# A gated cross-attention kernel: the last product of its setup split by a second Strassen step, and part of the setup's storing moved into the main loop

## The chip, the cores and the metric

The kernel runs on one core of a Trainium2 chip. The metric is the device time of one execution in microseconds (us); less is better. The time before is the median of three runs, 972.33 us (972.21 to 972.43). One further execution was recorded by the hardware profiler; every duration of a single instruction comes from there.

## The reference

All arrays are float32. Eight batches of 1024 rows x of width 1024 attend to 64 rows of memory of width 512.

```python
memory_proj = jnp.einsum('bme,de->bmd', memory, W_mem)            # "mp", 512 rows in all
scores = jnp.einsum('bnd,bmd->bnm', hidden_states, memory_proj) / jnp.sqrt(jnp.float32(D))
attn = jax.nn.softmax(scores, axis=-1)
memory_context = jnp.einsum('bnm,bmd->bnd', attn, memory_proj)
gate_input = jnp.concatenate([hidden_states, memory_context], axis=-1)
gate = jax.nn.sigmoid(jnp.einsum('bnf,df->bnd', gate_input, W_gate) + b_gate)
fused = hidden_states + gate * memory_context
return _rmsnorm(fused, norm_w)
```

W_gate acts on x by its first half, W1 (1024 x 1024), and on the context by its second half, W2. As the context is attn times mp, the kernel computes mp times W2 once ("mg", 512 x 1024) and uses attn times mg.

## The kernel before, in words

**Setup.** The weights and the memory are loaded; mp is computed, transposed, as four quarters m11, m12, m21, m22 (tiles mpT, each 128 x 4 x 256) by seven half-size products after Strassen (tiles pm). Then mg is computed from the quarters and from W2's eight tiles w2 (b11, b12, b21, b22 are column halves of four tiles each), again by seven products in Strassen's (Winograd's) form, in the order 1, 6, 5, 2, 7, 4, 3 (`mg_product`, `mg_sum`, tiles pg; lines 511 to 589). One such product is 8 matmuls of 128x512, into two PSUM banks. `setup_bank` (line 235) hands the eight banks out in turn. VectorE adds the products from PSUM into c11, c12, c21, c22, and `store_mg` writes these to a DRAM scratch tensor mgd[1]. The last product, 3, is s2 times b22 and goes into c12 alone. Between the products stand, by hand, the steps that prepare the main loop:

- `store_mp` (492, called at 550): for each of the four groups of 128 rows of mp, two VectorE transposes of 128x512 into a tile mpq, then four stores of 128 KB to mgd[0]. The mpq tiles take the tags it4, it6, it2, it3.
- `inner_sum` / `inner_sums` (217 to 224): for each of W1's seven outer operands (1 to 7), four sums of 128x512 that a second Strassen step needs, written to a tile it{o} and in place. Before the change GpSimd makes those of sets 1 (328), 7 (541), 5 (564), 6 and 4 (572); VectorE makes those of sets 2 and 3 in the first quad (645 to 648).
- `w2_sum` (321): b21 minus t2 on VectorE (569), four sums of 128x512, an operand of product 4.
- loading and transposing the first 512 rows of x (`load_xq`, `transpose_x`), and their first sums (`outer_s`, `inner_s`).

**Main loop.** A quad is 512 rows of x; there are 16, two to a batch (QPB = 2). A quad's product with W1 is seven outer products in the order 1, 6, 7, 5, 4, 2, 3 (`ORDER`), and each is seven inner products A, B, C, D, (A again), E, F of two matmuls of 128x256 (`outer_product`, line 758). An outer product has five banks for its kA to kF, and they rotate from one outer product to the next (898): kC takes the bank that kA of the outer product before had. Product A is copied out by ScalarE (815), and, for outer product 1, once more when its second half is in (810). The other sums are VectorE's (from PSUM) and GpSimd's (SBUF only). The last four outer products also add attn times mg (`ext`).

**Order of the work.** Every engine executes its instructions in the order of the program (`pin`). The steps beside the products are placed by hand: each inner product is a slot, a quad has 49, `at(slot, ...)` puts a step ahead of a slot, `mid` inside an outer product (`plan`, 607). Loads and stores other than the accumulating ones go through SyncE's queue (SP) in order. At a batch's start, `load_mg` (467) loads 64 rows of mgd[0] and mgd[1] into the tile mg, `load_mp` (463) those of mp, transposed, into the tile mpb, ten slots into the quad before.

**Buffers.** The pool `small` has one buffer for each tag. Tag junk is used by s3 in the setup (540), and in the quads by `square` (670): ScalarE squares a finished tile of 128 x 1024 into it, only for the sum. The squares of a quad's second row pair come in slots 3 and 4 of the next quad, those of the first pair in slots 17 and 18.

Of the kernel before, what the change touches and what calls it, by code (L numbers as in the profile page):

```python
# [8 lines left out]
F32 = mybir.dt.float32  # L9
AF = mybir.ActivationFunctionType  # L10
ALU = mybir.AluOpType
# [4 lines left out]
P = 128  # L16
# [4 lines left out]
def tile_gated_cross_attention_rmsnorm(  # L21
# [42 lines left out]
    nc = tc.nc  # L64
    B, N, D = x.shape
    M, E = mem.shape[1:]
    QT = 4 * P
    QPB = N // QT
    NQ = B * QPB
    BM = B * M  # L70
    KD = D // P
    KE = E // P
    H = 512
    C = 256
    NPAIR = BM // P
    SCALE = 1.0 / float(D) ** 0.5
    Q4 = D // 4

    const = ctx.enter_context(tc.tile_pool(name="const", bufs=1))
# [4 lines left out]
    small = ctx.enter_context(tc.tile_pool(name="small", bufs=1))  # L84
# [4 lines left out]
    pin = tc.keep_in_program_order  # L89

    def mm(o, lhsT, rhs, start, stop):
        pin(nc.tensor.matmul(o, lhsT, rhs, start=start, stop=stop, skip_group_check=True))  # L92

    def tt(eng, o, a, b, op):
        pin(eng.tensor_tensor(o, a, b, op))  # L95

    def load(o, i):
        pin(nc.sync.dma_start(o, i))

    def t4k(pool, shape, tag, name):  # L100
        return pool.tile(shape, F32, tag=tag, name=name)
# [5 lines left out]
    def chunks(t, n):  # L107

        return t.rearrange("p s e -> p (s e)").rearrange("p (m j) -> p j m", j=n)
# [26 lines left out]
    for k in range(KD):  # L136
        t = t4k(*((gpool, [P, D], "gate") if k < 7 else (apool, [P, D], "s4")), f"w2_{k}")
# [28 lines left out]
    def w1_place(o):  # L166

        if o in (5, 6, 4):
            outer_b[o] = const.tile([P, 4, H], F32, tag=f"t{o}", name=f"t{o}")
        inner_t[o] = const.tile([P, 3, 2, C], F32, tag=f"it{o}", name=f"it{o}")  # L170

    def w_op(o, s):
        if s >= T4:
            return inner_t[o][:, s - T4, :, :]
        k, n = {R11: (0, 0), R21: (1, 0), R12: (0, 1), R22: (1, 1)}[s]
        return outer_b[o][:, 2 * k : 2 * k + 2, n * C : (n + 1) * C]
# [8 lines left out]
    mgd = dram.tile([2, BM, D], F32, name="mgd")  # L185
# [31 lines left out]
    def inner_sum(eng, o, n):  # L217
        s, a, b = ((T1, R12, R11), (T2, R22, T1), (R12, R22, R12), (T4, R21, T2))[n]
        tt(eng, w_op(o, s), w_op(o, a), w_op(o, b), ALU.subtract)

    def inner_sums(eng, o):
        w1_place(o)
        for n in range(4):
            inner_sum(eng, o, n)
# [3 lines left out]
    KH = KD // 2  # L228
    HM = BM // 2
    mpT = [[t4k(apool, [P, KH, HM], f"a{r + 1}{h + 1}", f"mpT{r}{h}") for h in range(2)] for r in range(2)]  # L230
# [4 lines left out]
    def setup_bank(name):  # L235
        nonlocal setup_next
        tag = setup_banks[setup_next % 8]
        setup_next += 1
        return (ps_ctx if tag == "ctx" else ps).tile([P, H], F32, tag=tag, name=name)
# [54 lines left out]
    for k in range(2):  # L294
        pin(nc.scalar.copy(pw22[:, k], w22[:, k]))
    pgs = pm_product(2, w12, e21)
# [12 lines left out]
    pgs = pm_product(7, ps3, e12)  # L309
# [4 lines left out]
    b11, b12, b21, b22 = (  # L314
        [w2[h * KH + k][:, c * H : (c + 1) * H] for k in range(KH)]
        for h in range(2)
        for c in range(2)
    )
    t1, t2 = ([t[:, k, :] for k in range(KH)] for t in t_w2)

    def w2_sum(eng, o, a, b):
        for k in range(KH):
            tt(eng, o[k], a[k], b[k], ALU.subtract)
# [1 line left out]
    w2_sum(nc.gpsimd, t1, b12, b11)  # L325
    w2_sum(nc.gpsimd, t2, b22, t1)
    w2_sum(nc.gpsimd, b12, b22, b12)
    inner_sums(nc.gpsimd, 1)

    pgs = pm_product(3, ps4, e22)  # L330
    pm_sum(m21, m21, pgs)
# [4 lines left out]
    sTs, attns, attnTs, scs, mps, mgs = {}, {}, {}, {}, {}, {}  # L336
# [3 lines left out]
    def transpose_x(q, t, half):  # L340

        key = q, t // 2, half
        if key not in A:
            A[key] = t4k(
                apool, [P, KH, 2 * P], f"a{t // 2 + 1}{half + 1}", f"a{t // 2 + 1}{half + 1}_{q}"
            )
        r = t % 2
        pin(
            nc.vector.transpose(  # L349
                A[key][:, :, r * P : (r + 1) * P],  # L350
                chunks(xq[q][:, 4 * t : 4 * t + 4, :], KD)[:, half * KH : (half + 1) * KH],
            )
        )

    def outer_s(q, n):
        a11, a12, a21, a22 = (A.get((q, r, h)) for r in range(2) for h in range(2))
        if n == 3:
            S[q, 3] = a21
            tt(nc.vector, a21, a11, a21, ALU.subtract)
            return  # L360
        s = S[q, n] = t4k(apool, [P, KH, 2 * P], f"s{n}", f"s{n}_{q}")
        if n == 1:
            tt(nc.vector, s, a21, a22, ALU.add)
        elif n == 2:
            tt(nc.vector, s, S[q, 1], a11, ALU.subtract)
        else:
            tt(nc.vector, s, a12, S[q, 2], ALU.subtract)
# [13 lines left out]
    def quarters(l):  # L381
        return l[:, 0:2, 0:P], l[:, 2:4, 0:P], l[:, 0:2, P:], l[:, 2:4, P:]
# [106 lines left out]
        tt(eng, t, a, b, op)  # L489
        return t  # L490

    def store_mp(g):

        r, n = g // 2, g % 2
        mpq = const.tile([P, 4, Q4], F32, tag=f"it{(4, 6, 2, 3)[g]}", name=f"mpq{g}")
        for h in range(2):
            pin(
                nc.vector.transpose(
                    chunks(mpq, KD)[:, h * KH : (h + 1) * KH],
                    mpT[r][h][:, :, n * P : (n + 1) * P],  # L500
                )
            )
        for i in range(4):
            load(
                mgd[0, g * P : (g + 1) * P, i * Q4 : (i + 1) * Q4].rearrange(
                    "(s c) e -> c s e", c=32
                ),
                mpq[32 * i : 32 * (i + 1), :, :],
            )

    def mg_product(n, l, r):
        pgs = []
        for t in range(2):
            pg = setup_bank(f"pg{n}_{t}")
            for k in range(KH):
                mm(pg, l[:, k, t * P : (t + 1) * P], r[k], k == 0, k == KH - 1)
            pgs.append(pg)
        return pgs

    def mg_tile(pool, tag, name):  # L520
        return t4k(pool, [P, 2, H], tag, name)

    def mg_sum(o, a, pgs):
        for t in range(2):
            tt(nc.vector, o[:, t, :], a[:, t, :], pgs[t], ALU.add)
# [8 lines left out]
    s2 = mp_step(nc.vector, "s2", apool, s1, m11, ALU.subtract)  # L534
# [3 lines left out]
    outer_sum(7, 3, 7)  # L538
    w1_place(7)
    s3 = mp_step(nc.gpsimd, "junk", small, m11, m21, ALU.subtract)  # L540
    for n in range(4):
        inner_sum(nc.gpsimd, 7, n)
    c11 = mg_tile(rot, "u", "mg_c11")
    c12 = mg_tile(rot, "u", "mg_c12")
    c21 = mg_tile(rot, "l2", "mg_c21")
    c22 = mg_tile(small, "mg", "mg_c22")
    pgs = mg_product(1, m11, b11)
    for t in range(2):
        pin(nc.scalar.copy(c11[:, t, :], pgs[t]))
    for g in (2, 3, 0, 1):  # L550
        store_mp(g)
    load_mp(0)
    pgs = mg_product(6, s2, t2)
    mg_sum(c21, c11, pgs)
# [5 lines left out]
    pgs = mg_product(5, s1, t1)  # L560
# [1 line left out]
    w1_place(6)  # L562
    outer_sum(6, 3, 5)
    for n in range(4):
        inner_sum(nc.gpsimd, 5, n)
    pgs = mg_product(2, m12, b21)
    mg_sum(c11, c11, pgs)
    store_mg(c11, 0, 0)
# [8 lines left out]
    pgs = mg_product(7, s3, b12)  # L577
# [3 lines left out]
    pgs = mg_product(4, m22, b21)  # L581
    mg_sum(c21, c21, pgs)
    store_mg(c21, 1, 0)
    for t in (2, 3):
        transpose_x(0, t, 1)
    outer_s(0, 1)
    pgs = mg_product(3, s2, b22)
    mg_sum(c12, c12, pgs)
    store_mg(c12, 0, 1)
    outer_s(0, 2)  # L590
    load_mg(0)
# [5 lines left out]
    def at(slot, fn, *args):  # L597
        due.setdefault(slot, []).append(lambda: fn(*args))
# [8 lines left out]
    def plan(q):  # L607
        t0 = SLOTS * q
        nxt = q + 1 < NQ
        order = [o for o, _ in ORDER]  # L610
        for i, o in enumerate(order):
            for part, t in ((0, 1), (1, 2 if o == 7 else 5)):
                if i + 1 < len(order):
                    at(t0 + 7 * i + t, inner_s, q, order[i + 1], part)
                elif nxt:
                    at(t0 + 7 * i + t, inner_s, q + 1, order[0], part)
        if q == 0:
            at(t0 + 7, scores, q)
        at(t0 + (6 if q else 7), outer_s, q, 3)
        at(t0 + (20 if q else 7), outer_s, q, 4)  # L620
        at(t0 + 9, transpose_scores, q)
        at(t0 + 10, softmax_a, q)
        at(t0 + 13, softmax_b, q)
        at(t0 + 18, transpose_attn, q)
        at(t0 + 21, attn_difference, q)
        if not nxt:
            at(t0 + 5, load_last)
            return
        at(t0 + 2, load_xq, q + 1)
        for t in (2, 3):  # L630
            mid((q, 5), transpose_x, q + 1, t, 0)
            mid((q, 2), transpose_x, q + 1, t, 1)
        for i, t, half in ((36, 0, 0), (38, 1, 0), (42, 0, 1), (43, 1, 1)):
            at(t0 + i, transpose_x, q + 1, t, half)
        mid((q, 3), scores, q + 1)
        mid((q, 3), outer_s, q + 1, 1)
        mid((q, 3), outer_s, q + 1, 2)
        if (q + 1) % QPB == 0:
            at(t0 + 10, load_mp, (q + 1) // QPB)
            at(t0 + 49, load_mg, (q + 1) // QPB)  # L640
        if q == 0:
            at(t0 + 8, add_bias, mgs[0][M:P, :])
            at(t0 + 20, add_bias, mgd[1, M:, :])
# [290 lines left out]
```

## Time and profile before

| | |
|---|---|
| median of three runs | 972.33 us |
| the profiled execution: its own time | 972.56 us |
| its span in the trace | 970.8 us |
| TensorE matmuls busy | 959.5 us, 4986 records |
| VectorE busy | 818.4 us |
| GpSimd busy | 761.1 us |
| ScalarE busy | 328.5 us |
| granted TensorE clock | 0.996 |
| mg's products in the trace | 33.4 to 81.5 us |
| one quad | 54.85 us |

In the profile, PE is TensorE's matmuls, PEld its weight loads, DVE is VectorE, ACT ScalarE, POOL GpSimd, SP SyncE. A line of the timeline gives start, duration, engine, source line, operation, written tile <- read tiles, shape, and how many instructions were merged. One float32 matmul of the program appears as two records. Where a helper such as `tt` (line 95) or `mm` (line 92) issues the instruction, all its calls have the helper's line, and the tile names tell them apart. A bracket at the end is idle time of the engine just before, and what the profile takes to have ended it.

### The profile page before, as it was taken

What the parts mean: (1) busy time and instruction counts of PE and PEld (TensorE: products, weight loads), DVE (VectorE), ACT (ScalarE), POOL (GpSimd) and SP (SyncE); (2) the same over time, 40 slices, a digit from 0 to 9 for tenths busy, and PEclk for the clock granted to TensorE, in tenths of its full rate; (3) what the DMA queues carried; (4) which work ended last, traced back from release to release, by engine and by line L of the source; (5) the groups of instructions that cost most, each with busy time, mean ns of one, the idle gap of its engine ahead of it and who ended that gap; (6) DMA issues with size and microseconds to landing.
All of it is one profiled execution on the core that took longest, in us unless ns stands there. A gap on an engine that the chain in (4) does not pass through costs nothing.

```text
span 970.8 us, 14402 instructions
## 1 busy us (share of the span) xinstructions
PE 959.5 (99%) x4986; PEld 774.9 (80%) x4986; DVE 818.4 (84%) x1482; ACT 328.5 (34%) x604; POOL 761.1 (78%) x889
## 2 busy tenths in 40 slices
PE   9999999999999999999999999999999999999995
PEld 8646878788888888788888888888887878888884
DVE  6988879879797988979797978979797978979787
ACT  2000234161423334161433324152333425152345
POOL 4997878778786978878786978878687878878692
PEclk9999999999999999999999999999999999999998
DMA  9856573482919374482918375381917465391712
GB/s 378 271 141 163 98 131 98 114 169 72 178 66 166 97 144 105 108 176 66 184 65 159 102 137 113 95 188 55 195 67 146 115 129 121 87 196 48 189 69 86
DMA packets 70919, 128.32 MB, mean 132 GB/s; under 512 B 12352, under 2 KB 49216, under 8 KB 70592
## 3 DMA queue, kind: packets, MB, share of 16 engines
q1 hardware_dynamic: 61520, 93.34, 37.0%
q0 software_dynamic: 9184, 33.56, 18.9%
q8 instruction: 39, 0.64, 0.3%
q10 hardware_dynamic: 144, 0.52, 0.1%
q14 instruction: 32, 0.26, 0.1%
HBM read 87.56 MB, written 41.68 MB: 133 GB/s over the span
## 4 chain that ended last, share of the span: by engine, by line
PE 98%; DVE 1%; issue 0%; ACT 0%; DVEq 0%
PE kA L92 20%; PE pc L92 12%; PE kE L92 11%; PE kD L92 10%; PE kF L92 10%; PE kB L92 10%; PE kC L92 10%; PE psT L92 6%; PE pg L92 5%; PE pm L92 3%; PE pz L92 0%; PE pa L443 0%; PE sc L417 0%; PE pt L196 0%; DVE gate L749 0%
## 5 line engine op out<-in xcount | busy, mean ns | idle before, releaser
L95 POOL TENSOR_TENSOR gate<-gate,u 128x256 f32<-128x256 f32 x336 | 287.5, 887 | 107.5 <-DVE u L95 107.5
L662 ACT ACTIVATE gate<-gate 128x512 f32<-128x512 f32 x128 | 80.5, 631 | 306.9 <-DVE gate L95 306.1
L349 DVE STREAM_TRANSPOSE a<-xq 128x512 f32<-128x512 f32 x128 | 137.9, 1099 | 2.7 <-POOL it L95 2.7
L95 POOL TENSOR_TENSOR l<-a 128x256 f32<-128x256 f32 x128 | 122.0, 953 | 21.6 <-PE kA L92 20.4
L92 PE MATMUL pc<-mg,attnT 64*128 64x256 f32 x512 | 127.5, 389 | 0.0
L92 PE MATMUL kB<-it,l 128*128 128x256 f32 x448 | 115.1, 379 | 0.2 <-DVE gate L95 0.2
L92 PE MATMUL kD<-it,l 128*128 128x256 f32 x448 | 115.0, 379 | 0.0
L92 PEld LDWEIGHTS pc<-mg,attnT 64*128 64x128 f32 x512 | 90.6, 186 | 29.9 <-issue 21.2
L691 DVE SCALAR_TENSOR_TENSOR gate<-gate,ss,nw_sb 128x512 f32<-128x512 f32 x120 | 110.6, 931 | 1.1
L95 POOL TENSOR_TENSOR l<-s 128x256 f32<-128x256 f32 x96 | 78.0, 813 | 36.1 <-PE kF L92 35.9
L92 PE MATMUL kA<-w,a 128*128 128x256 f32 x384 | 98.6, 379 | 0.0
L92 PEld LDWEIGHTS kB<-it,l 128*128 128x128 f32 x448 | 85.0, 190 | 12.1 <-DVE gate L95 0.6
L92 PEld LDWEIGHTS kD<-it,l 128*128 128x128 f32 x448 | 85.1, 190 | 11.6
L95 DVE TENSOR_TENSOR gate<-gate,pc 128x512 f32<-128x512 f32 x128 | 86.7, 678 | 0.4 <-ACT gate L662 0.4
L95 DVE TENSOR_TENSOR gate<-gate,kE 128x256 f32<-128x256 f32 x112 | 45.5, 419 | 47.1 <-PE kE L92 41.1
L92 PEld LDWEIGHTS kA<-w,a 128*128 128x128 f32 x384 | 71.7, 190 | 9.5 <-DVE s L95 0.2
L815 ACT COPY u<-kA 128x256 f32<-128x256 f32 x112 | 40.5, 361 | 110.3 <-PE kA L92 106.0
L92 PE MATMUL kE<-it,a 128*128 128x256 f32 x256 | 69.0, 392 | 0.0
L676 ACT ACTIVATE junk<-gate 128x1024 f32<-128x1024 f32 x60 | 63.5, 1058 | 10.5 <-DMA gate<-in_x 9.5
L92 PE MATMUL kA<-t,s 128*128 128x256 f32 x256 | 65.8, 379 | 0.0
L92 PE MATMUL kC<-w,l 128*128 128x256 f32 x256 | 65.7, 379 | 0.0
L92 PE MATMUL kF<-w,l 128*128 128x256 f32 x256 | 65.7, 379 | 0.0
(140 smaller groups left out, 2041.0 us busy)
## 6 DMA issues: line engine op xcount, KB each, us to landing
xq<-in_x SPq DMA_DIRECT2D x64, 512.0 KB, 10.3
gate<-in_x POOLq DMA_DIRECT2D x60, 512.0 KB, 8.1
out<-gate SPq DMA_DIRECT2D x60, 512.0 KB, 2.6
w<-in_w_gate_t SPq DMA_DIRECT2D x8, 512.0 KB, 10.0
w<-in_w_gate_t SPq DMA_DIRECT2D x2, 2048.0 KB, 17.1
mg<-mgd SPq DMA_DIRECT2D x16, 256.0 KB, 3.8
mpd<-mpT SPq DMA_DIRECT2D x4, 512.0 KB, 7.0
mgd<-mpq SPq DMA_DIRECT2D x16, 128.0 KB, 3.6
```

Of the source, the lines that this page charges most:

```text
L92: pin(nc.tensor.matmul(o, lhsT, rhs, start=start, stop=stop, skip_group_check=True))
L95: pin(eng.tensor_tensor(o, a, b, op))
L349: nc.vector.transpose(A[key][:, :, r * P : (r + 1) * P], chunks(xq[q][:, 4 * t : 4 * t + 4, :], KD)[:, half * KH : (half + 1) * KH],)
L662: pin(nc.scalar.activation(g, g, AF.Sigmoid))
L676: nc.scalar.activation(junk, O[q, t], AF.Square, accum_out=ss[:, t % 2 : t % 2 + 1])
L691: nc.vector.scalar_tensor_tensor(g[:, cols], g[:, cols], rstd[:, t % 2 : t % 2 + 1], nw_sb[:, cols], ALU.mult, ALU.mult,)
L815: pin(nc.scalar.copy(p1, kb["A"]))
```

## The change

1. Product 3 of mg (s2 times b22, into c12) is made by a second Strassen step, `mg_nested`: twelve sums of 128x256 on GpSimd for its inputs (eight of b22's tiles, four of s2; they lie in buffers it2 and it3, whose W1 sums are made only in the quads), seven products of two matmuls of 128x256 into six banks, one ScalarE copy and three VectorE additions for the partial sums (tile mg_u, tag junk), three GpSimd additions into c12 and four VectorE additions into c12. The function is a generator run in three parts, with other work between.
2. Of mp's rows only group 0, the rows of batches 0 and 1, is transposed and stored in the setup (`store_mp_pair`). Those of batches 2 to 7 are made at slot 49 of the quad before the batch, that is, slot 0 of its first quad (`store_mp_batch`): one VectorE transpose of 128x512 from mpb into a tile mpq with tag junk, then four stores of 64 KB. `load_mg` moves one slot later and stands behind them.
3. W1's sums of sets 7 and 5 move from GpSimd to VectorE. Those of set 1 stay on GpSimd and move behind s3.

```diff
-    inner_sums(nc.gpsimd, 1)
...
-    def store_mp(g):
-
-        r, n = g // 2, g % 2
-        mpq = const.tile([P, 4, Q4], F32, tag=f"it{(4, 6, 2, 3)[g]}", name=f"mpq{g}")
+    def store_mp(mpq, rows):
+
+        for i in range(4):
+            load(
+                mgd[0, rows, i * Q4 : (i + 1) * Q4].rearrange("(s c) e -> c s e", c=32),
+                mpq[32 * i : 32 * (i + 1), :, :],
+            )
+
+    def store_mp_pair():
+        mpq = const.tile([P, 4, Q4], F32, tag="it4", name="mpq")
         for h in range(2):
             pin(
                 nc.vector.transpose(
-                    chunks(mpq, KD)[:, h * KH : (h + 1) * KH],
-                    mpT[r][h][:, :, n * P : (n + 1) * P],
+                    chunks(mpq, KD)[:, h * KH : (h + 1) * KH], mpT[0][h][:, :, :P]
                 )
             )
...
+        store_mp(mpq, slice(0, P))
+
+    def store_mp_batch(b):
+        mpq = t4k(small, [P, M // 32, Q4], "junk", f"mpq{b}")
+        pin(nc.vector.transpose(chunks(mpq, KD), mps[b]))
+        store_mp(mpq, slice(b * M, (b + 1) * M))
...
+    def mg_nested(eng, l, r, ts, ss, o):
+
+
+        l11, l12, l21, l22 = quarters(l)
+        s1_, s2_, s3_, s4_ = (ss[:, i] for i in range(4))
+        t1_, t2_, t3_, t4_ = (ts[i] for i in range(4))
+        lo, hi = slice(0, C), slice(C, H)
+        for k in range(2):
+            tt(eng, t1_[:, k, :], r[k][:, hi], r[k][:, lo], ALU.subtract)
+            tt(eng, t2_[:, k, :], r[2 + k][:, hi], t1_[:, k, :], ALU.subtract)
+            tt(eng, t3_[:, k, :], r[2 + k][:, hi], r[k][:, hi], ALU.subtract)
+            tt(eng, t4_[:, k, :], r[2 + k][:, lo], t2_[:, k, :], ALU.subtract)
+        tt(eng, s1_, l21, l22, ALU.add)
+        tt(eng, s2_, s1_, l11, ALU.subtract)
+        tt(eng, s3_, l11, l21, ALU.subtract)
+        tt(eng, s4_, l12, s2_, ALU.subtract)
+        yield
...
+        kb = [setup_bank(f"pn{i}")[:, :C] for i in range(6)]
+        ut = t4k(small, [P, 4, C], "junk", "mg_u")
+        p1_, u2, u3, u4 = (ut[:, i, :] for i in range(4))
...
+        product(0, l11, r11)
+        pin(nc.scalar.copy(p1_, kb[0]))
+        product(1, s2_, t2_)
+        add(u2, p1_, kb[1])
+        product(2, s3_, t3_)
+        add(u3, u2, kb[2])
+        for n in (3, 2):
+            tt(nc.gpsimd, dst[n], dst[n], u3, ALU.add)
+        product(3, s1_, t1_)
+        add(u4, u2, kb[3])
+        tt(nc.gpsimd, dst[1], dst[1], u4, ALU.add)
+        product(0, l12, r21, False)
+        product(4, l22, t4_)
+        product(5, s4_, r22)
+        yield
+        for n, b in ((0, 0), (3, 3), (2, 4), (1, 5)):
+            add(dst[n], dst[n], kb[b])
...
     s3 = mp_step(nc.gpsimd, "junk", small, m11, m21, ALU.subtract)
-    for n in range(4):
-        inner_sum(nc.gpsimd, 7, n)
+    inner_sums(nc.gpsimd, 1)
...
-    for g in (2, 3, 0, 1):
-        store_mp(g)
+    store_mp_pair()
+    for n in range(4):
+        inner_sum(nc.vector, 7, n)
     load_mp(0)
...
     outer_sum(6, 3, 5)
     for n in range(4):
-        inner_sum(nc.gpsimd, 5, n)
+        inner_sum(nc.vector, 5, n)
...
+    nested = mg_nested(
+        nc.gpsimd, s2, b22, [in_it2[:, 0], in_it2[:, 1], in_it2[:, 2], in_it3[:, 0]], ss3, c12
+    )
+    next(nested)
     pgs = mg_product(2, m12, b21)
...
+    next(nested)
     outer_s(0, 1)
-    pgs = mg_product(3, s2, b22)
-    mg_sum(c12, c12, pgs)
+    for _ in nested:
+        pass
     store_mg(c12, 0, 1)
...
         if (q + 1) % QPB == 0:
             at(t0 + 10, load_mp, (q + 1) // QPB)
-            at(t0 + 49, load_mg, (q + 1) // QPB)
+            if q + 1 > QPB:
+                at(t0 + 49, store_mp_batch, (q + 1) // QPB)
+            at(t0 + 50, load_mg, (q + 1) // QPB)
```

More of the change, by code (lines that the diff above doesn't have):

```diff
@@ L498, in store_mp @@
                 nc.vector.transpose(
-                    chunks(mpq, KD)[:, h * KH : (h + 1) * KH],
-                    mpT[r][h][:, :, n * P : (n + 1) * P],
-                )
-            )
[L503 to L509, printed above, removed]
+                    chunks(mpq, KD)[:, h * KH : (h + 1) * KH], mpT[0][h][:, :, :P]
+                )
+            )
+        store_mp(mpq, slice(0, P))
[3 more added lines that the diff above has]
+        store_mp(mpq, slice(b * M, (b + 1) * M))
     def mg_product(n, l, r):
@@ L518, in mg_product, with product, add @@
         return pgs
+    def mg_nested(eng, l, r, ts, ss, o):
[13 more added lines that the diff above has]
+        yield
+        r11, r22 = ([r[2 * h + k][:, n] for k in range(2)] for h, n in ((0, lo), (1, hi)))
+        r21 = [r[2 + k][:, lo] for k in range(2)]
+        t1_, t2_, t3_, t4_ = ([t[:, k, :] for k in range(2)] for t in (t1_, t2_, t3_, t4_))
+        kb = [setup_bank(f"pn{i}")[:, :C] for i in range(6)]
+        ut = t4k(small, [P, 4, C], "junk", "mg_u")
+        p1_, u2, u3, u4 = (ut[:, i, :] for i in range(4))
+        def product(n, left_, right_, start=True):
+            for k in range(2):
+                mm(kb[n], left_[:, k, :], right_[k], start and k == 0, k == 1)
+        dst = [o[:, t, n * C : (n + 1) * C] for t in range(2) for n in range(2)]
+        def add(to, a, b):
+            tt(nc.vector, to, a, b, ALU.add)
+        product(0, l11, r11)
[15 more added lines that the diff above has]
+            add(dst[n], dst[n], kb[b])
     def mg_tile(pool, tag, name):
@@ L564, in tile_gated_cross_attention_rmsnorm @@
     for n in range(4):
-        inner_sum(nc.gpsimd, 5, n)
+        inner_sum(nc.vector, 5, n)
+    in_it2, in_it3 = (
+        const.tile([P, 3, 2, C], F32, tag=f"it{o}", name=f"mg_it{o}") for o in (2, 3)
+    )
+    ss3 = in_it3[:, 1:].rearrange("p a k c -> p (a k c)").rearrange("p (i k m) -> p i k m", i=4, k=2)
+    nested = mg_nested(
+        nc.gpsimd, s2, b22, [in_it2[:, 0], in_it2[:, 1], in_it2[:, 2], in_it3[:, 0]], ss3, c12
+    )
+    next(nested)
     pgs = mg_product(2, m12, b21)
```

## The prediction, written before the changed kernel was run

> **What bounds the kernel now.** I read the page first: busy shares, then the chain that ended last.
>
> ```profile
> PE 959.5 (99%) x4986; PEld 774.9 (80%) x4986; DVE 818.4 (84%) x1482; ACT 328.5 (34%) x604; POOL 761.1 (78%) x889
> ...
> PE 98%; DVE 1%; issue 0%; ACT 0%; DVEq 0%
> ```
>
> TensorE is busy in 959.5 of 970.8 us and makes up 98% of the chain. So a matmul taken away is time gained, and anything that makes TensorE wait is time lost. VectorE and GpSimd have room on average only, so I read the stages that the change touches: the setup (30 to 90 us), then the start of a quad that opens a new batch. The timeline of the setup:
>
> ```profile
> 52.74 4.10 DVE L349 STREAM_TRANSPOSE a<-xq 128x512 f32<-128x512 f32 x4 [2.74 <-POOL it L95]
> ...
> 61.55 6.19 DVE L95 TENSOR_TENSOR w<-w,t_w 128x512 f32<-128x512 f32 x4
> ...
> 67.61 7.03 PE L92 MATMUL pg<-w,mpT 128*128 128x512 f32 x16
> ...
> 74.48 7.03 PE L92 MATMUL pg<-w,mp_s 128*128 128x512 f32 x16
> ...
> 78.67 2.19 DVE L95 TENSOR_TENSOR s<-a,a 128x1024 f32<-128x1024 f32 x1
> ...
> 83.07 1.03 PE L92 MATMUL kC<-w,l 128*128 128x256 f32 x4
> ```
>
> VectorE is the neighbour of the bound here: it waits once (2.74 us before 52.74) and is full otherwise. The four w sums make b21 for product 4, which starts at 67.61; they end at 67.74.
>
> The start of quad 4, on ScalarE, then TensorE, then VectorE (the quads that open batches 2 to 7 start alike, within 0.03 us):
>
> ```profile
> 306.50 1.06 ACT L676 ACTIVATE junk<-gate 128x1024 f32<-128x1024 f32 x1
> ...
> 307.68 1.06 ACT L676 ACTIVATE junk<-gate 128x1024 f32<-128x1024 f32 x1
> ...
> 308.85 1.28 ACT L681 ACT_TABLE_LOAD   x1
> ...
> 310.35 0.35 ACT L810 COPY gate<-kA 128x256 f32<-128x256 f32 x1
> ```
>
> ```profile
> 312.98 1.03 PE L92 MATMUL kC<-t,l 128*128 128x256 f32 x4
> ```
>
> ```profile
> 305.26 0.42 DVE L95 TENSOR_TENSOR gate<-gate,kF 128x256 f32<-128x256 f32 x1 [0.44 <-PE kF L92]
> 305.60 0.68 DVE L95 TENSOR_TENSOR gate<-gate,pc 128x512 f32<-128x512 f32 x1
> ```
>
> ScalarE squares two finished tiles into the buffer with tag junk, takes the root, and only then copies kA out of PSUM. The banks rotate so that kC of the next product (6) takes that bank. The copy ends at 310.70, kC comes at 312.98: 2.28 us of room. The stores that the change moves, from the view of the tile mpq and the DMA view of 53 to 58 us:
>
> ```profile
> L98 SPq DMA_DIRECT2D mgd<-mpq x16: 303/430/522, 43.3 to 56.3; - x16
> ...
> DMA to landing us min/median/max: 2.4/3.6/9.6
> ```
>
> ```profile
> mgd<-mpq SPq DMA_DIRECT2D x8, 128.0 KB, 2.6
> ```
>
> 0.43 us to issue one, and 2.6 us to land where the DMA engines are not full.
>
> [...] no mpq store landed in under 2.4 us, so a smaller store is not a much quicker one. [...] w sums beside a busy GpSimd took 6.19/4 = 1.55 us, sums of the same size at 84.48 with GpSimd idle took 0.68. [...] In the trace each engine's instructions follow the program's order, so what is behind a waiting one waits too.
>
> **The change, part by part.**
>
> *TensorE.* Product 3 was 16 records of 0.429 us = 6.87 us. Seven small products replace it, each 0.864 us (kB at 82.21 to kC at 83.07): 6.05 us. Gain 0.82 us, on the path.
>
> *VectorE in the setup.* Six of eight mpq transposes go (0.96 us each, 7.70/8); eight 128x512 sums of sets 7 and 5 come. One such sum costs 0.68 us (GpSimd idle) to 1.55 (the w sums). I take 1.1, half of the 2.19 of the 128x1024 sum at 78.67, which also had GpSimd busy. The four of set 7 are free: two transposes, four sums even at 1.55, and product 6's sums (1.29) take 9.4 us from 41.19, ending at 50.6, before the data of xq let VectorE go on at 52.74. The four of set 5 come after that point and before the w sums: +4.4 us. Last w sum then ends at 67.74 + 4.4 = 72.1; its first use is product 4's fourth pair of records, at 67.61 + 3 x 0.86 = 70.2. TensorE waits 2.0 us there. Further on, VectorE was done with the sum s at 80.78; now 4.4 later, plus three additions of partial products ahead of s (3 x 0.42) and the first last addition to c12 (0.42): 86.9. That addition frees the bank that kC of quad 0 takes. TensorE would be there at 74.48 + 2.0 + 6.05 + 1.73 = 84.3 and waits for 86.9. So kC starts 86.9 - 83.07 = 3.8 us later than before; this net shift already holds the 0.82 gained and the wait at product 4. The ends: 0.68 a sum gives +2.1, 1.55 gives +5.6. A gain is excluded unless xq lands earlier.
>
> *GpSimd in the setup.* Eight sums of 1.27 go (10.2 us); twelve inputs and three additions of 128x256 come, 15 x 0.72 to 0.95 = 11 to 14 us; set 1 moves behind s3. Priced at nothing: the inputs are started at about 58 and end by 70, product 3's place is 77; if that cover goes, each us late is a us of TensorE. The bank kC waits for needs no GpSimd addition. ScalarE's one extra copy (0.37) meets an idle engine.
>
> *SP in the setup.* 12 stores of 128 KB go, 5.2 us of issue; the first loads of mp and x keep their place. Nothing on the path.
>
> *Batch starts.* Six times, VectorE transposes one mpb (1.10, as for xq) right behind the kF sum: 305.60 to 306.70. The following VectorE work is pushed by 1 us, and 0.71 + 0.31 + 0.98 of its idle time in the next 5 us takes that up. SP then issues four stores of 64 KB: the last at 306.70 + 0.05 + 3 x 0.43 = 308.05. Their price is not in the trace at this size: lower end 2.4 (least of the 128 KB ones), upper 3.6 (their median, most of them beside full DMA engines). I take 2.6, for the load of x is now behind them and does not compete. They land at 310.65. The transposed rows lie in the buffer with tag junk, so ScalarE's first square, free to go at 306.50 before, waits for all four stores. Behind it in ScalarE's queue are the second square, the root with its table, the copy of kA, and the next product's copy. First square to end of the kA copy is 310.70 - 306.50 = 4.20, so the bank is free at 314.85; TensorE comes at 312.98 and waits 1.87 us. Ends: 1.7 to 2.9. Six of them: 11.2 us (10.2 to 17.3).
>
> *SP at batch starts.* The load of mg, and the load of x behind it, wait for the stores: mg issued at 310.7 instead of 299.69, x from 311.7. The last x part lands about 313.3 + 10.5 (its median in that window) = 323.8; VectorE wants it at 328.52 + 1.9. mg is wanted at 327.97. Covered by 6 us; were x later than that, each us would reach TensorE through VectorE.
>
> **Sum.** Against the profiled execution's own 972.56 (span 970.8 and 1.76 around it): + 3.8 + 11.2 = 987.6. The median of the runs, 972.33, is 0.2 lower: 987.3.
>
> **The rivals.**
> 1. *Setup covered, batch starts as priced.* [...] xq, with fewer stores beside it, lands 2 us earlier. Against: the stores beside it were mostly issued after it. 972.3 + 11.2 - 0.8 = 982.7.
> 2. *Stores or x land late.* The read and accumulate of x by GpSimd's DMAs (issued 306.7 and 308.3, 11.5 us to land in that window) share the engines with the stores: 3.6 to land, 2.9 us of wait, 17.3 in all, setup at its upper end: 995.2; x landing at its longest (18.3 us in the whole trace) would add over 1 us each.
> 3. *Not slower: DMAs land early.* If the stores release ScalarE by 312.98 - 4.20 = 308.8, that is within 0.7 us of the last issue, the batch starts cost nothing, and xq in by 50.6 leaves 1.7 us of the setup: 974.0. It decides at that 0.7 us; no store in the trace is near it.
> 4. *Batch starts covered, setup as priced:* 972.3 + 3.8 = 976.1.
>
> **How the numbers follow.** Forecast 0.64; rival 1 0.14; rival 2 0.12; rival 3 0.04; rival 4 0.06. The rivals 3 and 4 lie below 979 (0.10), part of rival 2 above 996 (under 0.07), so the range is 979 to 996. About 0.2% is what a measurement of this kernel can tell from no change (970.4 to 974.3). Faster 0.01, same 0.05 (rival 3 and a little of the others), slower 0.94.
>
> **What would show it.** In the profile after: ScalarE's junk square waiting some 4 us for a DMA at quads 4, 6, 8, 10, 12, 14, and kC of product 6 some 2 us late right after, with no such gap at odd quads; TensorE waits near 70 and before kC of quad 0 for VectorE; pn matmuls of 6.05 us together. I am wrong if the squares start within 2.3 us of their old place, if VectorE reaches the c12 additions before 83, or if TensorE waits elsewhere, for xq above all.

## The result and the profile after

| | before | changed | ratio, 95% interval |
|---|---|---|---|
| median | 972.38 us (6 runs) | 1019.87 us (1017.67 to 1021.43, 6 runs) | 1.0488 [1.0477, 1.0499] |
| profiled execution | 972.56 us, span 970.8 | 1017.67 us, span 1015.8 | |

The changed kernel is 47.5 us slower: 1019.87 us, where 987.3 was forecast, with a range to 996. The direction was right; the forecast rise of 15 us was under a third of the real one.

The page of the changed kernel: the shares of busy time, and the chain that ended last.

```profile
PE 975.3 (96%) x4998; PEld 783.8 (77%) x4998; DVE 828.6 (82%) x1495; ACT 328.5 (32%) x605; POOL 766.0 (75%) x896
...
PE 80%; DMA 8%; DVE 4%; POOL 3%; issue 3%; ACT 2%; SPq 1%; DVEq 0%; ACTq 0%; POOLq 0%
```

Two things are to be seen. TensorE has fallen from 98% of the chain to 80%, and DMA, which was not in the chain at all, has 8%. And TensorE is busy 15.8 us longer (959.5 before) though its work became smaller: it must have run slower at times. The granted clock, averaged over the run, is 0.983 (0.996 before).

Where the 45.0 us of span lie can be read from the starts of psT, the scores, once in a quad, in the chain in order of time. To the psT in quad 0, 2.2 us are added, and the psT of the next quad stands at 137.36 instead of 135.08 us (+2.28). Six intervals between two psT, those that hold a batch start with stores, take 61.59 to 62.50 us instead of 54.85 to 55.04: together +42.5. The other intervals are unchanged, and the stretch behind the last psT grows by 0.2. So six batch starts cost 7.1 us each, where 1.9 was forecast, and the setup costs 2.3, where 3.8 was forecast.

The start of quad 4, ScalarE and then TensorE, answering to the lines at 306.50 to 310.35 and at 312.98 of before (this run is 2.3 us later here):

```profile
314.39 1.06 ACT L741 ACTIVATE junk<-gate 128x1024 f32<-128x1024 f32 x1 [5.50 <-DMA mgd<-mpq]
...
318.24 0.35 ACT L875 COPY gate<-kA 128x256 f32<-128x256 f32 x1
```

```profile
318.73 2.05 PE L92 MATMUL kC<-t,l 128*128 128x256 f32 x4 [3.30 <-ACT gate L875]
320.57 1.61 PE L92 MATMUL kD<-it,l 128*128 128x256 f32 x4
322.01 1.03 PE L92 MATMUL kA<-t,s 128*128 128x256 f32 x4
...
333.26 0.91 PE L92 MATMUL kB<-it,l 128*128 128x256 f32 x3 [1.36 <-DVE gate L95]
```

The forecast wait is there: the square waits for the mpq stores, and kC of product 6 for the copy behind it. But it is 3.3 us, not 1.87. Then kC and kD start 1.84 and 1.44 us apart, where each product of this size took 0.86 before: a slow TensorE costs 1.55 us more. And 11 us later TensorE waits again, at kB of product 5, for VectorE. What VectorE waited for stands in the chain in order of time:

```profile
310.35 3.94 DMA mgd<-mpq
...
323.36 9.00 DMA out<-gate
```

The first line is the last of the four mpq stores: 3.94 us to land. The second is a store of a finished tile (the "out store" from here on), 9.00 us to land; only then is its gate buffer free for VectorE's next sums:

```profile
332.45 0.42 DVE L95 TENSOR_TENSOR gate<-gate,kA 128x256 f32<-128x256 f32 x1 [2.53 <-DMA out<-gate]
```

The same store in the kernel before, and VectorE's use of the buffer behind it, without a wait:

```profile
out<-gate SPq DMA_DIRECT2D x1, 512.0 KB, 4.9
```

```profile
322.04 0.42 DVE L95 TENSOR_TENSOR gate<-gate,kA 128x256 f32<-128x256 f32 x1
```

The clock is in the view by stretches (stretch, length, busy time of PE, PEld, DVE, ACT, POOL, granted clock, DMA share, GB/s). Of the stretch behind the first wait, part was at half the clock (granted clock 0.50 from 318.32 to 321.73):

```profile
320.00:325.00 5.00, 5.00 (x20) 4.24 (x20) 4.06 (x11) 0.58 (x2) 3.63 (x5) 0.83 1.15 191
325.00:330.00 5.00, 5.00 (x25) 4.36 (x25) 4.13 (x7) 4.26 (x8) 4.92 (x7) 1.00 1.17 198
```

Quad 4 is one of six such starts. At the others the first wait is 3.34 to 3.54 us, the slow products behind it lose 1.8 to 3.1 us, and the second wait is 0.1 to 1.8 us. Over all six: 20.5 us of first wait, 12.9 of slow clock, 5.5 of second wait. These three can't simply be added up as causes, as the experiments show.

### The profile page after: what moved, and what is told of

It is laid out like the page before. It is cut to its first block, busy times and chain, and to the rows that moved or that the text cites. A ratio compares the mean times of both kernels' runs of the same rounds, so it can differ in the third digit from the quotient of the medians.

```text
span 1015.8 us, 14492 instructions
## 1 busy us (share of the span) xinstructions
PE 975.3 (96%) x4998; PEld 783.8 (77%) x4998; DVE 828.6 (82%) x1495; ACT 328.5 (32%) x605; POOL 766.0 (75%) x896
## 4 chain that ended last, share of the span: by engine, by line
PE 80%; DMA 8%; DVE 4%; POOL 3%; issue 3%; ACT 2%; SPq 1%; DVEq 0%; ACTq 0%; POOLq 0%
PE kA L92 16%; PE pc L92 12%; PE kE L92 9%; PE kC L92 9%; PE kD L92 9%; PE kB L92 8%; PE kF L92 8%; PE psT L92 6%; DMA out<-gate 5%; PE pm L92 2%; DMA mgd<-mpq 2%; POOL mg_it L95 2%; DMA xq<-in_x 1%; POOL it L95 1%; ACT junk L741 1%
## 5 line engine op out<-in xcount | busy, mean ns | idle before, releaser
L95 POOL TENSOR_TENSOR l<-a 128x256 f32<-128x256 f32 x128 | 117.1, 915 | 24.5 <-PE kA L92 20.9
L92 PE MATMUL kD<-it,l 128*128 128x256 f32 x448 | 119.5, 391 | 0.0
L92 PEld LDWEIGHTS kD<-it,l 128*128 128x128 f32 x448 | 88.1, 197 | 12.8
L95 DVE TENSOR_TENSOR u<-u,kB 128x256 f32<-128x256 f32 x112 | 45.4, 406 | 40.6 <-ACT u L880 26.8
L92 PE MATMUL kC<-t,l 128*128 128x256 f32 x192 | 53.9, 406 | 20.5 <-ACT gate L875 20.5
L92 PE MATMUL kA<-t,s 128*128 128x256 f32 x256 | 69.6, 396 | 0.0
```

## Experiments

Each is a change to the changed kernel unless said otherwise. All ratios are to the kernel before on the same chip.

**e1: a buffer of its own for the batch tile.**

```diff
-        mpq = t4k(small, [P, M // 32, Q4], "junk", f"mpq{b}")
+        mpq = t4k(small, [P, M // 32, Q4], "mpq", f"mpq{b}")
```

> The batch tile mpq gets a buffer of its own instead of the one with tag junk; nothing else differs from the changed kernel. Theory A (two separate waits at each of six batch starts: first ScalarE's square waits for the four mpq stores and kC of product 6 with it, then the load of x, issued late behind the stores, delays the out store and with it a gate buffer): the first wait (3.3 us and the slow clock after it, some 5 us each) goes, the second stays or grows, as the out store is no longer delayed with everything else: 985 to 1000 us. Theory B (the second wait only follows from the first): both go, about 975 us. Theory C (the added stores and transposes cost wherever they stand): about 1018 us.

Measured: 1031.67 us, ratio 1.0616 [1.06, 1.0631]. Taking the forecast wait away made the kernel 11.8 us slower. Its squares start as early as in the kernel before (1.5 us after the quad), and the wait at kC is gone. The second wait, TensorE and then VectorE:

```profile
333.52 2.07 PE L92 MATMUL kB<-it,l 128*128 128x256 f32 x4 [6.60 <-DVE gate L95]
335.39 1.67 PE L92 MATMUL kC<-t,l 128*128 128x256 f32 x4
```

```profile
332.71 0.42 DVE L95 TENSOR_TENSOR gate<-gate,kA 128x256 f32<-128x256 f32 x1 [8.35 <-DMA out<-gate]
```

The out store is now issued at 319.09, without the delay of the first wait, and takes 13.5 us to land. It lands at nearly the same time as in the changed kernel (332.62 and 332.36). So the out store's landing holds TensorE, whatever happens before it: in both kernels kB of product 5 starts 0.9 us after that landing, at all six starts. The first wait only used up time that TensorE would otherwise have spent in the second. What makes e1 slower than the changed kernel is the slow clock: it now comes behind the last wait, where nothing hides it, and costs 1.6 to 2.7 us a start, 13.5 in all. Theory A's "stays or grows" is right, but 985 to 1000 us was too low; theory B has fallen.

**e2: as e1, and the stores and the load of mg behind the load of x.**

```diff
-                at(t0 + 49, store_mp_batch, (q + 1) // QPB)
-            at(t0 + 50, load_mg, (q + 1) // QPB)
+                at(t0 + 53, store_mp_batch, (q + 1) // QPB)
+            at(t0 + 54, load_mg, (q + 1) // QPB)
```

> As e1, and the stores (slot 53) and the load of mg (slot 54) stand behind the load of x in SP's queue. Theory A: neither wait is left, only the setup's cost: 974 to 976 us. Theory B: the same as e1. Theory C: about 1018 us.

Measured: 977.92 us, ratio 1.0056 [1.0041, 1.0071], 2 us above what was expected. Both waits are gone at most batch starts; two of them still take 0.6 us more than other quads. The mpq stores, behind x, take 6.5 us to land (median), and nobody waits for them. This is read from the quickest of the four runs (976.24 us), the one that was profiled.

**e3: the stores at slot 30 of the quad before, still with tag junk.**

```diff
-                at(t0 + 49, store_mp_batch, (q + 1) // QPB)
+                at(t0 + 30, store_mp_batch, (q + 1) // QPB)
```

> The tile mpq keeps tag junk, but the transpose and its stores stand at slot 30 of the quad before the batch, between the squares of slots 17 and 18 and those of the next quad. Theory A: 974 to 976 us. Theory C: 1010 to 1020 us, since the same work is still in the quads.

Measured: 975.7 us, ratio 1.0038 [1.0025, 1.0051]. The same transposes, stores and buffer, 19 slots earlier, cost next to nothing. Theory C (the added work itself) has fallen.

**e4: TensorE kept busy during the first wait.**

```diff
+        if o == 6 and q >= 4 and q % QPB == 0:
+            pw = ps_ctx.tile([P, H], F32, tag="ctx", name=f"pw{q}")
+            for _ in range(8):
+                mm(pw[:, :C], ident, nw_sb[:, :C], True, True)
         product("C", 2, s3, R12)
```

> The changed kernel with 8 more matmuls of 128x256 (3.4 us) that nobody reads, ahead of kC of product 6 at quads 4, 6, 8, 10, 12 and 14, where TensorE otherwise idles 3.3 us. If TensorE is clocked down because it idled (theory A), kC and kD after the wait take 0.86 us each instead of 1.84 and 1.44, and the run is 6 x 1.6 = 9 us shorter: about 1010 us. If the lower clock has another cause, no shorter: 1018 to 1022 us.

Measured: 1024.41 us, ratio 1.0541 [1.0524, 1.0557]: the expected gain in time is missed. The clock, though, did what was expected:

```profile
315.69 3.62 PE L92 MATMUL pw<-nw_sb,ident 128*128 128x256 f32 x16
...
319.78 1.10 PE L92 MATMUL kC<-t,l 128*128 128x256 f32 x4 [0.25 <-ACT gate L875]
...
333.75 1.13 PE L92 MATMUL kB<-it,l 128*128 128x256 f32 x4 [2.29 <-DVE gate L95]
```

kC and kD now take 0.93 and 0.87 us. The time won is lost again 10 us later, at kB: that wait ends when the out store has landed, whatever TensorE did before. The run is even 4.5 us longer than the changed kernel, 6.5 in the two traces. Of these 6.5 us, 4.4 are slow products behind the second wait, at quads 8, 10 and 14, where it is now 3.61, 3.20 and 2.84 us long; 1.5 are out stores that land later, and 0.6 lie in the setup.

**e8: the same in e1, where only the second wait is left** (15 such matmuls ahead of kB of product 7).

```diff
+        if o == 7 and q >= 4 and q % QPB == 0:
+            pw = ps_ctx.tile([P, H], F32, tag="ctx", name=f"pw{q}")
+            for _ in range(15):
+                mm(pw[:, :C], ident, nw_sb[:, :C], True, True)
         product("B", 1, s2, T2)
```

> e1 (mpq with a buffer of its own) with 15 matmuls of 128x256 (6.4 us) that nobody reads ahead of kB of product 7 at the six batch starts, where e1 leaves TensorE idle for some 6.6 us and then runs kB and kC in 1.87 and 1.51 us. If the slow clock comes from the idle time and costs 1.7 us each, the run is 10 us under e1: about 1021 us. If not: 1031 us.

Measured: 1018.36 us, ratio 1.0475 [1.0461, 1.0489], 13.3 us under e1. The expectation names the place wrongly: in e1 the wait is at kB of product 5, so the added matmuls stood some 6 us before it and moved TensorE's arrival behind nearly all of it. The two kernels between 330 and 335 us, e1 first (columns as above):

```profile
330.00:335.00 5.00, 1.48 (x4) 1.21 (x5) 2.29 (x4) 0.00 (x0) 2.14 (x3) 0.50 0.57 211
```

```profile
330.00:335.00 5.00, 4.98 (x24) 4.04 (x24) 3.36 (x7) 2.04 (x6) 2.81 (x4) 1.00 0.80 250
```

Between 330 and 335 us TensorE has half its clock in e1 (granted clock 0.50), all of it in e8 (1.00). 13.3 us over six starts are 2.2 each, and the slow products of e1 account for it: 1.6 us at quad 4 (kB and kC in 1.87 and 1.51 us), up to 2.7 at the others, 13.5 together. kB of product 5 still starts 0.9 us behind the landing of the out store. So e8 takes about what the changed kernel takes: the same landing, and no slow clock behind it.

**e12: the load of x ahead of the stores, mpq with tag junk.**

```diff
-        at(t0 + 2, load_xq, q + 1)
+        if q < 4 or q % QPB:
+            at(t0 + 2, load_xq, q + 1)
...
+                at(t0 + 49, load_xq, q + 2)
                 at(t0 + 49, store_mp_batch, (q + 1) // QPB)
```

> The changed kernel (tag junk) with the load of the next quad's x ahead of the stores in SP's queue at the six batch starts; the load of mg stays behind the stores. Theory A: the out store is on time again and only the first wait is left, at kC of product 6, with the slow clock after it: about 5 us at each start, 1002 to 1008 us; more, up to 1020 us, if the stores land later behind x (6.5 us in e2) and ScalarE's square waits longer for them. If the second wait were the first one's follower (theory B): 1018 us, as the changed kernel.

Measured: 1024.96 us, ratio 1.0549 [1.0532, 1.0567], over the upper end of what was expected. The last mpq store, from the chain, and what TensorE then waits for:

```profile
310.17 8.21 DMA mgd<-mpq
```

```profile
322.82 2.04 PE L92 MATMUL kC<-t,l 128*128 128x256 f32 x4 [7.56 <-ACT gate L877]
```

No wait for an out store is left among this kernel's longest waits: at this start it lands in 2.6 us. The wait for the mpq stores has grown from 3.3 to 7.6 us at quad 4, and from 20.5 to 33.6 over the six starts. With tag junk at slot 49 there is no good order: with the stores first the out store is late, with x first ScalarE is. Of the four combinations of buffer and order only the one that frees both, e2, is quick (its stores stand at slot 53, so it isn't e12 with the buffer alone changed).

**e7: the kernel before with the moved stores alone** (part 2 of the change; product 3 and W1's sums as before).

```diff
...
-    for g in (2, 3, 0, 1):
-        store_mp(g)
+    store_mp_pair()
...
-            at(t0 + 49, load_mg, (q + 1) // QPB)
+            if q + 1 > QPB:
+                at(t0 + 49, store_mp_batch, (q + 1) // QPB)
+            at(t0 + 50, load_mg, (q + 1) // QPB)
```

> The kernel before with the moved stores alone: rows of batches 2 to 7 at slot 49 with tag junk, load of mg at slot 50; product 3 and the W1 sums as before. If the batch starts cost by themselves what they cost in the changed kernel, some 7 us each, 1012 to 1017 us. If the setup's parts had a share in it, less than 1005 us.

Measured: 1016.09 us, ratio 1.0453 [1.0438, 1.0467]. The moved stores alone cost 43.8 us, of the 47.5 of the whole change.

**e11: e7 with the stores at slot 30**, by the one line of e3's diff.

> e7 (the kernel before with the moved stores alone) with the stores at slot 30. The batch starts cost nothing there; the setup has six VectorE transposes and 12 stores less but TensorE was not waiting for them: 971.8 to 972.6 us.

Measured: 972.25 us, ratio 1.0001 [0.9993, 1.0009]: no difference. So it is the place of the stores that costs, not the stores.

**e5, e6, e9, e10: what the smaller product costs in the setup.** All start from e3. In the setup of the changed kernel, VectorE, TensorE, and VectorE again:

```profile
66.09 4.10 DVE L95 TENSOR_TENSOR w<-w,t_w 128x512 f32<-128x512 f32 x4
```

```profile
67.02 7.79 PE L92 MATMUL pg<-w,mpT 128*128 128x512 f32 x16
...
83.87 1.13 PE L92 MATMUL kC<-w,l 128*128 128x256 f32 x4 [1.30 <-DVE mg_c L95]
...
88.64 1.13 PE L92 MATMUL kF<-w,l 128*128 128x256 f32 x4 [1.05 <-DVE u L95]
```

```profile
85.33 0.42 DVE L95 TENSOR_TENSOR mg_c<-mg_c,pn 128x256 f32<-128x256 f32 x1 [1.51 <-POOL mg_c L95]
```

Product 4 is 0.76 us longer than before (7.03), kC waits, and kF waits for a VectorE that itself waited for GpSimd. e5 moves GpSimd's sums of set 4 out of the way, into slots 0, 6, 6 and 19 of quad 0:

```diff
-    for o in (6, 4):
-        for n in range(4):
-            inner_sum(nc.gpsimd, o, n)
+    for n in range(4):
+        inner_sum(nc.gpsimd, 6, n)
...
+    for n, s in enumerate((0, 6, 6, 19)):
+        at(s, inner_sum, nc.gpsimd, 4, n)
```

> e3 (stores at slot 30), and GpSimd's four sums of set 4 move out of the setup into quad 0 (slots 0, 6, 6, 19), so that its three additions into c12 come some 5 us earlier. If GpSimd's additions hold VectorE and with it kF of quad 0 (theory D), the 1.2 us wait there goes and the run is about 974.5 us; if VectorE's own load is the whole of the setup's cost (the prediction's view), no change: 975.7 us.

Measured: 976.22 us, ratio 1.0042 [1.0028, 1.0055]. The wait at kF is gone, as theory D has it, and the time is not: quad 0 now loses more, at kB and kC of product 7 and around product 5. e6 also moves VectorE's sums one place back:

```diff
-    for n in range(4):
-        inner_sum(nc.vector, 5, n)
...
-    for i, (o, n) in enumerate((o, n) for o in (2, 3) for n in range(4)):
-        at((3, 4, 5, 6, 22, 23, 24, 25)[i], inner_sum, nc.vector, o, n)
+    for i, (o, n) in enumerate((o, n) for o in (5, 2, 3) for n in range(4)):
+        at((3, 4, 5, 6, 22, 23, 24, 25, 29, 30, 31, 32)[i], inner_sum, nc.vector, o, n)
```

> e5, and VectorE's sums move one place back: set 5 into slots 3 to 6 of quad 0, set 2 to 22 to 25, set 3 to 29 to 32. That takes 4.5 us of VectorE out of the setup ahead of b21. If the waits at product 4 (0.8 us) and at kC of quad 0 (1.5 us) come from there, both go and only the smaller product remains: 971.5 to 972 us, just under the kernel before. If VectorE is then late in quad 0 instead: 974 to 977 us.

Measured: 973.9 us, ratio 1.0017 [1.0011, 1.0024]. TensorE waits nowhere in the setup and begins quad 0 at 80.33 us, 1.02 before the kernel before. It then loses 1.1 us up to kE of product 5 (110.15 instead of 110.06) and 1.2 more up to kE of product 4, both times for VectorE's sums. e9 puts GpSimd's four sums where GpSimd idles (two ahead of its additions into c12, two at slot 0) and the last four of VectorE at slots 33, 34, 36 and 37; e10 also puts one sum of set 5 into VectorE's idle time before the first data of x. The diff of e9 to e3, and then of e10 to e9:

```diff
-    for n in range(4):
-        inner_sum(nc.vector, 5, n)
...
-    for o in (6, 4):
-        for n in range(4):
-            inner_sum(nc.gpsimd, o, n)
+    for o, n in ((6, 0), (6, 1), (6, 2), (6, 3), (4, 0), (4, 1)):
+        inner_sum(nc.gpsimd, o, n)
...
-    for i, (o, n) in enumerate((o, n) for o in (2, 3) for n in range(4)):
-        at((3, 4, 5, 6, 22, 23, 24, 25)[i], inner_sum, nc.vector, o, n)
+    for i, (o, n) in enumerate((o, n) for o in (5, 2, 3) for n in range(4)):
+        at((3, 4, 5, 6, 22, 23, 24, 25, 33, 34, 36, 37)[i], inner_sum, nc.vector, o, n)
+    for n in (2, 3):
+        at(0, inner_sum, nc.gpsimd, 4, n)
```

```diff
     mg_sum(c21, c11, pgs)
+    inner_sum(nc.vector, 5, 0)
...
-    for i, (o, n) in enumerate((o, n) for o in (5, 2, 3) for n in range(4)):
-        at((3, 4, 5, 6, 22, 23, 24, 25, 33, 34, 36, 37)[i], inner_sum, nc.vector, o, n)
+    for i, (o, n) in enumerate((o, n) for o in (5, 2, 3) for n in range(o == 5, 4)):
+        at((3, 4, 5, 6, 22, 23, 24, 25, 33, 34, 36)[i], inner_sum, nc.vector, o, n)
```

> From e3: GpSimd's sums of set 4 go where it idles (two ahead of its additions into c12, two at slot 0); VectorE's sums of set 5 into slots 3 to 6 of quad 0, set 2 to 22 to 25, set 3 to 33, 34, 36, 37. e6 reached quad 0 a microsecond early and lost 2.2 us within it, at kE and kB of outer products 5 and 4. If that came from GpSimd's late sums and from VectorE's sums at slots 29 to 32, the loss goes: 971.4 to 972 us. If VectorE cannot take four more sums anywhere in quad 0: 973 to 974.5 us.

> As e9, but one sum of set 5 stands in the setup where VectorE waits for the first data of x (1.7 us in the changed kernel), and the others move up by one place. If that idle time takes it for nothing, equal to e9 or up to 0.7 us under it; if it delays VectorE's transposes of x, up to 1 us over.

Measured: e9 973.8 us, ratio 1.0016 [1.0009, 1.0023]; e10 974.68 us, ratio 1.0028 [1.0018, 1.0038]. Both lie above the kernel before. The loss in quad 0 only moves: e9 begins quad 0 1.2 us early and is 1.2 us late by kE of product 2. In four placements I found none that gains; that there is none isn't shown. No version beat the kernel before.

## Why the prediction was wrong, step by step

**TensorE's gain: right.** The small products run from 74.64 to kA at 80.68: 6.04 us, 6.05 forecast.

**The setup: within its ends, partly wrong in its working.** 3.8 us forecast (2.1 to 5.6), 2.3 measured (e3 is 3.2 over the kernel before). VectorE's four sums of set 5 took 1.10 to 1.21 us (1.1 forecast), and the waits at product 4 and at kC came where they were forecast. They are smaller (0.76 instead of 2.0, 1.3 instead of 2.6), mostly because the w sums behind took 4.10 us and not 6.19. GpSimd's sums beside them were now of 128x256 (1.05 to 1.17 us each), before of 128x512 (1.59 to 1.71); whether that made the difference was not tested. "GpSimd in the setup, priced at nothing" failed: I asked when its inputs for the small products were due, not when its additions behind them were. Its queue, with sets 6 and 4 between, reached these only at 84.57, and that is the wait at kF (1.05), which e5 takes away.

**The batch starts: the place right, three terms wrong.**

1. *Landing.* The step "I take 2.6 ... They land" holds for the issue (the last store starts 3.07 us after the quad; 3.06 forecast) and for the chain behind (4.20 us, as forecast). The landing was mis-sized. The first three stores landed in 1.7 to 1.8 us, under the lower end, and the last in 3.94, over the upper one (3.90 to 4.17 at the six starts). The residual loads of x on GpSimd's queue were issued at 309.83 and 310.74, in between; at slot 30 (e3), without them, five of the six last stores landed in 1.73 to 1.80, one in 3.50. I had taken a median where the wait ends with the last of four. The step "a smaller store is not a much quicker one" rested on stores of 128 KB alone, none of which landed in under 2.4 us, and did not hold: the first store of 64 KB, with no packet of another transfer in the view when it was issued (309.0 to 309.2), landed in 1.7 us.

2. *The clock.* No step priced what TensorE does after a wait. The forecast wait was 1.9 us, the real one 3.3. In the traces the granted clock is 0.50 around the end of a wait of 6.6 us (e1, 330 to 335 us), kC and kD take 1.55 us longer behind 3.3 us, and nothing is lost behind 2.3 us (e4). They show no sharp limit: in those of the changed kernel, e1, e4, e7 and e12, no wait of up to 2.79 us was followed by slow products, 13 of the 16 between 2.84 and 3.68 us were, and all 14 from 3.80 us up. What decides it between 2.84 and 3.68 us was not shown. The stretches at half clock at the six starts of the changed kernel last 3.41 us (four) and 6.83 us (two). In the changed kernel the slow products are over before the second wait ends, so quick ones gained nothing there (e4); in e1, behind the last wait, it cost 13.5 us.

3. *"SP at batch starts. Covered by 6 us."* This is the step that failed and that set the size. I followed the load of x to its reader, who had time, and stopped there. The queue goes on behind it: SP issued, in the kernel before and then in the changed one,

```profile
300.88 2.13 SPq L98 DMA_DIRECT2D xq<-in_x  x4
...
316.77 5.66 SPq L98 DMA_DIRECT2D out<-gate  x2
```

```profile
315.53 2.48 SPq L98 DMA_DIRECT2D xq<-in_x  x4
...
323.36 6.96 SPq L98 DMA_DIRECT2D out<-gate  x2
```

x is 2 MB. Issued 12 us later (the quad itself is 2.3 later here), it is still under way when the next out store comes. (SP issued mg's load, with x behind it, at 314.36, when the last mpq store had landed at 314.29, so the mis-sized landing delays x too. The last part of x landed at 331.11, which is 328.8 on the clock of the kernel before; 323.8 was forecast, again with a median where the last of four counts. Its reader still did not wait.) The runs show that the out store lands after x: it landed in 9.0 us (13.5 in e1), median 2.6 over the whole run, and at all six starts of the changed kernel and of e1 it landed 0.9 to 1.3 us behind the last part of x. With x ahead of the stores (e12) it landed in 2.6 us. Why it waits for x was not shown. In the kernel before that store landed at 321.7, and VectorE used the buffer from 322.04. The cover that was broken was 0.4 us for VectorE, not 6. For TensorE it was some 1.8 us, an estimate: kB of product 5 stood 2.7 us behind the landing, and 0.9 us is what the path from the landing to kB takes in the changed kernel. The landing came 8.4 us later, and 6.5 of them reached kB.

Over the six starts kB of product 5 comes 40.7 us later, of the 42.5 that the batch starts cost. So an exact forecast of the first wait would not have mended the sum: e1, without that wait, is slower still. Rival 2 named late stores and a late x, with x's reader as the one who waits; it is nearer, and wrong in that. Even its 995 us was outside what came.

The two waits taught me something too: they are not additive. Taking away the first alone (e1) leaves the second at its place and exposes the slow clock behind it; taking away the second alone (e12) makes the first longer. Judged by either run alone, each wait would have seemed to cost nothing.

## What to carry to other kernels

Of a DMA that is moved or delayed, follow the queue, not only the reader: ask which transfer comes behind it, how full the queue then is, and who needs the buffer that it frees. A buffer shared by tag with a step on another engine makes that engine wait for a DMA's completion (ScalarE 5.50 us at quad 4), so put such a store where the next user is far away. 19 slots earlier (e3) both the buffer and the queue were free, and 44 us were won. Where waits follow one another, price the one that ends last. And on this kernel, 98% TensorE, slow products stood behind 13 of the 16 waits of 2.84 to 3.68 us and behind all 14 longer ones; they cost time where no later wait hides them (13.5 us in e1).

## What the hardware did that I had not expected

After 3.3 us of idling TensorE took 1.84 and 1.44 us for two products of 0.86; after 7.6 us (e12) three were slow (1.83, 1.71, 1.47). With useless matmuls in the gap they ran at 0.93 and 0.87. But two waits of 3.18 and 3.68 us (e7) were followed by full speed, and one of 2.84 us (e4) was not. The same store of 64 KB landed in 1.7 us with no other transfer in the view (the first of the four), in 3.94 as the last of four beside residual loads, in 4.6 to 5.1 with x ahead of it, and in 8.21 as the last of four with both (e12, quad 4).
